# A graph layer on one core: edge groups of 8 columns, 5 gathered by Pool and 3 by TensorE, with window sums over 48 nodes

## The chip, the cores and the metric

The kernel runs on one core of a Trainium2 chip. The metric is the device time of one execution in microseconds. It is the median of the runs shown; a profiled execution of the same kernel gives the page and the trace.

## What is computed

There are 6250 nodes with 64 features and 206250 edges, sorted by the node that they point to. The features are normalized and cut at zero (h). Every edge takes the row of h at its source node, adds its own attributes and cuts at zero; the results are summed by destination, and a small two-layer network works on h plus the sum.

```python
h = jnp.maximum(_layernorm(x, axis=-1), 0.0)
msg = jax.nn.relu(h[src] + edge_attr)
agg = jax.ops.segment_sum(msg, dst, num_segments=x.shape[0])
y = h + agg
y = jax.nn.relu(y @ W1 + b1)
out = x + (y @ W2 + b2)
```

## The kernel before

**Groups.** The sorted edges are cut into groups of 128 x G edges, G = 6: a group is a tile of 128 partitions by 6 columns by 64 features. There are NG = 268 whole groups and a tail of four columns. For each edge two things are needed: the row of h at its source, and the place of its destination.

**Two ways to get the source rows.** Of each group the first G - H = 3 columns are gathered by Pool: one indirect DMA a column (`gather`, L175) brings 128 rows from `h_rows` in HBM into `xg`. The last H = 3 columns are fetched by TensorE from a copy of h that stays in SBUF (`hp`, three bf16 parts whose sum is the f32 value). It works in sets of two groups and in two steps. In the first (`slots_of`, L417), 56 matmuls a group select the wanted nodes of each of 28 parts into 32 slots a part, with the three parts side by side, 192 columns; ScalarE casts the result from PSUM to bf16 (`slots_out`, L425, tile `picked`). In the second (`pick`, L434), the way back, matmuls with the one-hot tile `backs` put each slot's row at its edge. Each of the 3 columns takes 7 x 3 = 21 matmuls of 64 columns, since the three parts are accumulated one after the other into the same 64 columns of PSUM. The one-hot tiles are made by VectorE (`find` L394, `back` L403) from tables that SP's queue loads (`source_load`, `spot_load`).

**One group's sum.** `messages(g)`: VectorE adds the gathered rows to the attributes (L478) and the picked rows to the other columns (L480); ScalarE cuts at zero (L482). `one_hot(g)` compares the edges' destinations with the W = 32 nodes that follow the group's first one (L464). `window_sum(g)` multiplies messages and one-hot on TensorE (L492) into a slice of the PSUM tile `agg`; one such tile holds AB = 4 groups and two tiles take turns. `sum_into_z(g)` adds the slice into z on VectorE, at an address read from the destinations (L458).

**Order.** The order of the work is written out by hand. After a start in which h is made (x is loaded, normalized, turned, split into parts) while RAW = 5 groups are gathered as raw rows of x and normalized by themselves, `half(g)` is called for every later group. Each call issues, in this order: the loads of group g + AHEAD (SP's queue for the attributes, Pool for the gathers; the pool of buffers holds LOOK = 12 groups, AHEAD = 9), a table load, `window_sum(g-1)`, the first part of `slots_of` for the next set, `sum_into_z(g-2)` and the output blocks that have become ready, `messages(g)`, `pick(g+1)` for two columns, the rest of `slots_of`, `pick(g+1)` for the third, `one_hot(g)`, and the one-hot tiles and ranking for later sets. Each engine does its own part of that list in order and waits where it needs another's result. PSUM holds two tiles each of `pick`, `half`, `rows` and `agg`.

At the end, a loop over edges that did not fit a window or a slot runs if there are any (`all_windows`).

Of the kernel before, what the change touches and what calls it, by code (L numbers as in the profile page):

```python
# [9 lines left out]
F32 = mybir.dt.float32  # L10
# [5 lines left out]
ALU = mybir.AluOpType  # L16
AX = mybir.AxisListType
DVE = mybir.EngineType.DVE

N, E, D = 6250, 206250, 64  # L20
P = 128
G = 6
GE = P * G
NG = E // GE
TE = E - NG * GE
# [3 lines left out]
TD = TJ * P - (TE - P)  # L29
C = NG * G  # L30
CT = TJ + 1
CP = C + G
W = 32
WB = 512
R = 4
NB = N // (P * R)
TN = N - NB * P * R
EPS = 1e-5
LOOK = 12
AHEAD = 9  # L40
LAG = 2
AB = 4
RV = 16

H = 3
# [6 lines left out]
S = 32  # L52
Q = PARTS * S // P
XC = 14
RAW = 5
F0 = RAW
KS = (NG + 1 - F0) // 2
assert F0 + 2 * KS == NG + 1
# [11 lines left out]
def kernel(  # L70
# [14 lines left out]
    nc = tc.nc  # L85
    ctx.enter_context(tc.manual_schedule())

    const = ctx.enter_context(tc.tile_pool(name="const", bufs=1))
    edge = ctx.enter_context(tc.tile_pool(name="edge", bufs=LOOK))
    work = ctx.enter_context(tc.tile_pool(name="work", bufs=2))  # L90
    rank = ctx.enter_context(tc.tile_pool(name="rank", bufs=2))
    dram = ctx.enter_context(tc.tile_pool(name="dram", bufs=1, space=bass.MemoryType.DRAM))
    psum = ctx.enter_context(tc.tile_pool(name="psum", bufs=2, space=bass.MemoryType.PSUM))

    src_sb = const.tile([P, CP], I32, name="src_sb")
    dst_sb = const.tile([P, CP], I32, name="dst_sb")
    FIRST = (F0 + 2 * 2 * SETS) * G
    nc.sync.dma_start(out=src_sb[:, :FIRST], in_=src_main[:, :FIRST])
# [60 lines left out]
    h_rows = dram.tile([NP, D], F32, name="h_rows")  # L159
    z = const.tile([P, N + W], F32, name="z")  # L160
    nc.vector.memset(z[D:], 0.0)
    nc.vector.memset(z[:D, N:], 0.0)

    def attr_load(ea, g):
        if g < NG:
            nc.sync.dma_start(out=ea.rearrange("p j d -> p (j d)"),
                              in_=edge_attr[g * GE:(g + 1) * GE, :].rearrange("(p j) d -> p (j d)", j=G))
        else:
            nc.sync.dma_start(out=ea[:, G - CT:G - 1].rearrange("p j d -> p (j d)"),
                              in_=edge_attr[C * P:(C + TJ) * P, :].rearrange("(p j) d -> p (j d)", j=TJ))  # L170
            nc.sync.dma_start(out=ea[:, G - 1, :], in_=edge_attr[E - P:, :])

    def gather(xg, idx, n, rows):
        for j in range(n):
            nc.gpsimd.indirect_dma_start(  # L175
                out=xg[:, j, :], out_offset=None, in_=rows[:, :],
                in_offset=bass.IndirectOffsetOnAxis(ap=idx[:, j:j + 1], axis=0))

    def first_col(g):
        return 0 if g < NG else G - CT  # L180

    def pool_cols(g):
        return G - H if g >= F0 else G

    def load(g):
        ea = edge.tile([P, G, D], F32, name="ea")
        attr_load(ea, g)
        lo, hi = first_col(g), pool_cols(g)
        if g < RAW:
            xg = lnp.tile([P, G, D], F32, name="xr", bufs=RAW)  # L190
        else:
            xg = edge.tile([P, G - H, D], F32, name="xg")
        gather(xg[:, lo:], src_sb[:, g * G + lo:g * G + hi], hi - lo, x if g < RAW else h_rows)
        return ea, xg

    def cols_of(g):
        return slice(g * G + first_col(g), (g + 1) * G)

    loaded = [load(g) for g in range(RAW)]

# [139 lines left out]
    def find_left(i):  # L340
# [3 lines left out]
        nc.vector.tensor_scalar(lf, sl, 1.0, None, op0=ALU.is_lt)  # L344
        nc.vector.scalar_tensor_tensor(lf, sl, float(W), lf, op0=ALU.is_gt, op1=ALU.add)
        nc.vector.scalar_tensor_tensor(lf, dst_sb[:, lo:hi], 1.0, lf, op0=ALU.add, op1=ALU.mult)
# [22 lines left out]
    def window_start(g):  # L369
        if g % RV == 0:  # L370
            n = min(RV, NG + 1 - g)
            _, vals = nc.values_load_multi_w_load_instructions(
                dst_sb[0:1, g * G:(g + n - 1) * G + 1:G], engines=(DVE,), min_val=0, max_val=N - 1,
                skip_runtime_bounds_check_because="dst holds numbers of nodes")
            for k, v in enumerate(vals):
                starts[g + k] = v
        return starts.pop(g)

    backs, sources, spots, found, picked, halves, picks = {}, {}, {}, {}, {}, {}, {}

    def source_load(k):
        sources[k] = rank.tile([P, PARTS * 2 * S], I16, name="sources")
        nc.sync.dma_start(out=sources[k][:PP], in_=lines[k // SETS][k % SETS].rearrange("(o m) s -> o (m s)", o=1)
                          .to_broadcast([PP, PARTS * 2 * S]))
# [41 lines left out]

    def pick(g, cols):
        k, i = divmod(g - F0, 2)
        if cols[0] == 0:
            picks[g] = psum.tile([P, H, D], F32, name="pick", bufs=2)  # L430
        for u in cols:
            for q in range(Q):
                for t in range(3):
                    nc.tensor.matmul(picks[g][:, u], backs[k][:, q, i * H + u, :],  # L434
                                     picked[k][:, i * Q + q, t * D:(t + 1) * D],
                                     start=(q == 0 and t == 0), stop=(q == Q - 1 and t == 2))

    def norm_edges(xg):
        s = work.tile([P, G], F32, name="raw_s")
# [11 lines left out]
        nc.vector.scalar_tensor_tensor(xg, xg, 0.0, v.unsqueeze(2).to_broadcast([P, G, D]),  # L451
                                       op0=ALU.max, op1=ALU.mult)

    aggs, hots, taken, msgs, banks = {}, {}, {}, {}, []

    def sum_into_z(g):
        at = window_start(g)
        nc.vector.tensor_tensor(z[:, ds(at, W)], z[:, ds(at, W)], aggs.pop(g), ALU.add)  # L458

    def one_hot(g):  # L460
        lo = first_col(g)
        n = G - lo
        oh = work.tile([P, G, W], F32, name="oh")
        nc.vector.tensor_tensor(  # L464
            oh[:, lo:], slot[:, cols_of(g)].unsqueeze(2).to_broadcast([P, n, W]),
            slots[:, :W].unsqueeze(1).to_broadcast([P, n, W]), ALU.is_equal)
        hots[g] = oh

    def enter(g):
        if g <= NG and g not in taken:  # L470
            taken[g] = loaded[g] if g < RAW else load(g)

    def messages(g):
        lo, m = first_col(g), pool_cols(g)
        ea, xg = taken.pop(g)
        if g < RAW:
            norm_edges(xg)
        nc.vector.tensor_tensor(ea[:, lo:m], ea[:, lo:m], xg[:, lo:m], ALU.add)  # L478
        if m < G:
            nc.vector.tensor_tensor(ea[:, m:], ea[:, m:], picks.pop(g), ALU.add)  # L480
        msg = work.tile([P, G, D], F32, name="msg", bufs=3)
        nc.scalar.activation(msg[:, lo:], ea[:, lo:], AF.Relu)  # L482
        msgs[g] = msg

    def window_sum(g):
        lo, oh, msg = first_col(g), hots.pop(g), msgs.pop(g)
        if g % AB == 0:
            banks.append(psum.tile([P, AB, W], F32, name="agg", bufs=2))
        pa = banks[-1][:, g % AB]
        for j in range(lo, G):  # L490
            i = (j - lo) % 2
            nc.tensor.matmul(pa[i * D:(i + 1) * D], msg[:, j, :], oh[:, j, :], start=(j < lo + 2), stop=(j >= G - 2))  # L492
        aggs[g] = pa
# [55 lines left out]
    def is_set(k):  # L549
        return 0 <= k < KS  # L550

    def half(g):
        k, i = divmod(g - F0, 2)
        first = ((0, 2), (8, 10))[i]
        later = ((4, 6), (12,))[i]
        now = is_set(k + 1)
        enter(g + AHEAD)
        if i == 0:
            if is_set(k + 3):
                source_load(k + 3)  # L560
        elif is_set(k + 3):
            spot_load(k + 3)
        if g >= 1:
            window_sum(g - 1)
        if now:
            for n0 in first:
                slots_of(k + 1, n0)
                slots_out(k + 1, n0)
        if g >= LAG:
            sum_into_z(g - LAG)  # L570
            blocks_behind(g - LAG)
        messages(g)
        if g < NG:
            pick(g + 1, (0, 1))
        if now:
            for n0 in later:
                slots_of(k + 1, n0)
                slots_out(k + 1, n0)
        if g < NG:
            pick(g + 1, (2,))  # L580
        one_hot(g)
        if i == 0:
            if is_set(k + 1):
                back(k + 1, 4, Q)
            if is_set(k + 2):
                find(k + 2, 0)
        else:
            if is_set(k + 2):
                back(k + 2, 0, 4)
                find(k + 2, 1)  # L590
        at = g - F0
        chunk(at + 14, rank_at)
        chunk(at + 13, rank_count)
        chunk(at + 12, rank_of)
        chunk(at + 11, rank_marks)
        chunk(at + 11, rank_turn)
        chunk(at + 10, rank_holds)
        chunk(at + 10, rank_fits)
        chunk(at + 9, source)
        if g in CHECKS:  # L600
            find_left(CHECKS.index(g))
# [50 lines left out]
    rank_fits(0)  # L652
    for g in range(AHEAD):
        enter(g)
# [4 lines left out]
    for g in range(RAW):  # L659
        enter(g + AHEAD)  # L660
        messages(g)
# [30 lines left out]
        slots_out(0, n0)  # L692
    source_load(2)
    spot_load(2)
    pick(F0, (0, 1, 2))
    find(1, 0)
    find(1, 1)
    back(1, 0, 4)
# [25 lines left out]
    with tc.If(any_left > 0):  # L724
        with tc.For_i(0, NG, 1) as i:
# [4 lines left out]
            ea = edge.tile([P, G, D], F32, name="ea")  # L730
# [5 lines left out]
        ea = edge.tile([P, G, D], F32, name="ea")  # L736
# [46 lines left out]
```

## Time and profile before

| | |
|---|---|
| Median of 3 runs | 2159.18 us (2152.33 to 2159.98) |
| Profiled execution | 2166.87 us |
| Span of its instructions | 2165.2 us |
| Mean granted clock of TensorE | 0.81 |
| Busy: PE, PEld | 1587.4, 1246.3 us |
| Busy: DVE, ACT, POOL | 964.1, 598.1, 864.5 us |
| Matmuls | 35792 |
| Instruction fetch queue q8 | 282 transfers, 4.62 MB |

PE is TensorE's matmuls and PEld its weight loads, which overlap them; DVE is VectorE, ACT ScalarE, POOL GpSimd, SP the engine whose queue issues most loads. The span runs from the first instruction to the last. In a row of the profile stand the line of the code, the engine and operation, the tiles written and read, the shapes and the count; then busy time and the mean of one in ns; then the idle time of the engine just before these instructions and what ended most of it. "Issue" as the end of a wait means that the profile shows nothing that was waited for. Matmuls are pipelined, so the mean of one (207 ns for L434) is a latency and not the pace of a stream; the pace is read from how long a row of many takes in the timeline.

### The profile page before, as it was taken

The numbers are of one execution on the slowest core, as the hardware profiler recorded it, in microseconds if no ns is written. First come the engines' busy times: TensorE is split into PE (matmuls) and PEld (weight loads), VectorE is DVE, ScalarE is ACT, GpSimd is POOL, SyncE is SP. The second block draws the span as 40 slices with busy tenths as digits, with TensorE's granted clock in tenths as the row PEclk, the third lists the DMA queues.
The fourth block names the chain that finished last, engine by engine and source line by source line (L and its number), as shares of the span: only waits on it lengthen the run. The fifth ranks groups of instructions, "written<-read, shape, count | busy, mean of one in ns | idle before, by whom it ended". The sixth has DMA issues, their size and how long they took to land.

```text
span 2165.2 us, 79562 instructions
## 1 busy us (share of the span) xinstructions
PE 1587.4 (73%) x35792; PEld 1246.3 (58%) x35792; DVE 964.1 (45%) x2721; ACT 598.1 (28%) x1351; POOL 864.5 (40%) x834
## 2 busy tenths in 40 slices
PE   1147787787778777777787778778777777778788
PEld 0135565565556655665565666556665566556566
DVE  7074443444444344444344444444444444444445
ACT  1132222232223222223222223222222322223223
POOL 7514433434444344434433443344434434443330
PEclk9998887777878788878778778777778987888779
DMA  5113233223333233333322323232323322323321
GB/s 165 29 47 88 73 95 81 71 75 83 78 81 88 80 74 77 88 79 88 83 72 76 88 72 90 75 85 74 89 71 82 96 76 70 89 77 91 81 77 35
DMA packets 112983, 172.67 MB, mean 80 GB/s; under 512 B 29185, under 2 KB 83585, under 8 KB 112637
## 3 DMA queue, kind: packets, MB, share of 16 engines
q1 hardware_dynamic: 85534, 139.02, 21.8%
q0 software_dynamic: 26240, 26.92, 7.5%
q8 instruction: 282, 4.62, 0.9%
q10 hardware_dynamic: 864, 1.60, 0.2%
q14 instruction: 63, 0.52, 0.1%
HBM read 163.56 MB, written 3.88 MB: 77 GB/s over the span
## 4 chain that ended last, share of the span: by engine, by line
PE 71%; issue 21%; another core or an unknown queue 3%; DVE 2%; DMA 2%; ACT 0%; DVEq 0%; POOL 0%; SPq 0%; ACTq 0%
PE pick L434 34%; PE half L417 25%; PE agg L492 8%; DMA x_sb<-in_x_dram 1%; PE rows L279 1%; PE rows L509 1%; PE rows L240 1%; PE rows L238 1%; PE rows L520 1%; PE rows L267 0%; DVE backs L403 0%; ACT z L318 0%; DVE found L394 0%; DVE rest L325 0%
## 5 line engine op out<-in xcount | busy, mean ns | idle before, releaser
L175 POOL DMA_INDIRECT xg<-h_rows,src_sb x790 | 831.1, 1052 | 1227.2 <-DVE ea L480 907.1
L434 PE MATMUL pick<-picked,backs 128*128 128x64 bf16 x16632 | 773.6, 207 | 245.3 <-issue 239.0
L434 PEld LDWEIGHTS <-backs 128*128 128x128 bf16 x16632 | 650.9, 107 | 412.4 <-issue 401.7
L425 ACT CAST picked<-half 128x384 bf16<-128x384 f32 x924 | 420.6, 480 | 1380.6 <-PE half L417 888.9
L417 PE MATMUL half<-hp,found 112*32 112x192 bf16 x14784 | 595.2, 283 | 196.9 <-issue 186.6
L417 PEld LDWEIGHTS <-found 112*32 112x32 bf16 x14784 | 379.6, 109 | 304.0 <-issue 267.7
L458 DVE TENSOR_TENSOR z<-z,agg 128x32 f32 x269 | 49.9, 185 | 714.1 <-PE agg L492 694.0
L403 DVE TENSOR_SCALAR backs<-spots,ids 128x768 bf16<-128x768 int16 x924 | 327.7, 414 | 0.0
L480 DVE TENSOR_TENSOR ea<-ea,pick 128x192 f32<-128x192 f32 x264 | 92.2, 349 | 407.7 <-PE pick L434 380.8
L492 PE MATMUL agg<-oh,msg 128*64 128x32 f32 x3224 | 187.9, 256 | 10.6 <-issue 8.1
L492 PEld LDWEIGHTS agg<-oh,msg 128*64 128x64 f32 x3224 | 153.2, 172 | 44.1 <-issue 27.8
L394 DVE TENSOR_SCALAR found<-sources,nodes_of 112x1792 bf16<-112x1792 int16 x264 | 178.0, 675 | 0.1
L482 ACT ACTIVATE msg<-ea 128x384 f32<-128x384 f32 x269 | 142.7, 530 | 5.3 <-DVE ea L478 3.0
L464 DVE TENSOR_TENSOR oh<-slot,slots 128x192 f32<-128x192 int16 x269 | 94.4, 351 | 0.0
L478 DVE TENSOR_TENSOR ea<-ea,xg 128x192 f32<-128x192 f32 x264 | 93.6, 355 | 0.7
L317 PE MATMUL rows<-ident,x_sb 112*64 112x112 f32 x56 | 12.7, 394 | 49.9 <-issue 42.5
L238 PE MATMUL rows<-at,upper 128*128 128x504 bf16 x44 | 25.7, 585 | 22.8 <-DVE at L232 21.5
L317 PEld LDWEIGHTS rows<-ident,x_sb 112*64 112x64 f32 x56 | 7.7, 160 | 55.2 <-issue 45.9
L279 PE MATMUL rows<-holds,marks 128*28 128x32 bf16 x792 | 29.5, 185 | 11.3 <-DVE holds L257 5.9
L175 POOL DMA_INDIRECT xr<-in_x_dram,src_sb x30 | 31.1, 1035 | 10.6 <-issue 8.8
L279 PEld LDWEIGHTS <-marks 128*28 128x28 bf16 x792 | 24.2, 100 | 15.5 <-DVE holds L257 6.0
L257 DVE TENSOR_TENSOR holds<-rank_of,from 128x576 bf16<-128x576 f32 x44 | 32.9, 749 | 0.0
(94 smaller groups left out, 391.3 us busy)
## 6 DMA issues: line engine op xcount, KB each, us to landing
sources<-source_row SPq DMA_DIRECT2D x132, 392.0 KB
ea<-in_edge_attr_dram SPq DMA_DIRECT2D x268, 192.0 KB
spots<-spot_rows SPq DMA_DIRECT2D x132, 192.0 KB
xg<-h_rows,src_sb POOLq DMA_INDIRECT x790
h_rows<-x_sb SPq DMA_DIRECT2D x4, 392.0 KB
x_sb<-in_x_dram SPq DMA_DIRECT2D x4, 388.5 KB
xb<-in_x_dram SPq DMA_DIRECT2D x12, 128.0 KB
out_dram<-o SPq DMA_DIRECT2D x12, 128.0 KB
```

The source lines that it names most:

```text
L175: nc.gpsimd.indirect_dma_start(out=xg[:, j, :], out_offset=None, in_=rows[:, :], in_offset=bass.IndirectOffsetOnAxis(ap=idx[:, j:j + 1], a ...
L279: nc.tensor.matmul(ps[:, i], mk[:, i * H + t, :], oh[:, i * H + t, :], start=(t == 0), stop=(t == H - 1))
L394: nc.vector.tensor_scalar(found[k][:PP, b].rearrange("p m i s -> p (m i s)"), sources[k][:PP], nodes_of[:PP, b:b + 1], None, op0=ALU.is_equal)
L403: nc.vector.tensor_scalar(backs[k][:, q].rearrange("p t s -> p (t s)"), spots[k].bitcast(I16), ids[:, q:q + 1], None, op0=ALU.is_equal)
L417: nc.tensor.matmul(ps[j * S:(j + 1) * S, u], found[k][:PP, b, m, i, :], hp[:, b * PARTS + m].rearrange("p t d -> p (t d)"), start=(b == 0) ...
L425: nc.scalar.copy(picked[k][:, n0:n0 + 2], halves.pop((k, n0)))
L434: nc.tensor.matmul(picks[g][:, u], backs[k][:, q, i * H + u, :], picked[k][:, i * Q + q, t * D:(t + 1) * D], start=(q == 0 and t == 0), st ...
L464: nc.vector.tensor_tensor(oh[:, lo:], slot[:, cols_of(g)].unsqueeze(2).to_broadcast([P, n, W]), slots[:, :W].unsqueeze(1).to_broadcast([P, ...
L478: nc.vector.tensor_tensor(ea[:, lo:m], ea[:, lo:m], xg[:, lo:m], ALU.add)
L480: nc.vector.tensor_tensor(ea[:, m:], ea[:, m:], picks.pop(g), ALU.add)
L482: nc.scalar.activation(msg[:, lo:], ea[:, lo:], AF.Relu)
L492: nc.tensor.matmul(pa[i * D:(i + 1) * D], msg[:, j, :], oh[:, j, :], start=(j < lo + 2), stop=(j >= G - 2))
```

## The change

Groups have 8 columns: NG becomes 201, with the same tail of four columns. Pool gathers 5 columns of each group and TensorE still fetches 3. The window is 48 nodes wide. Four groups are raw. LOOK is 9 and AHEAD 6.

On the way back, the three bf16 parts are no longer accumulated into the same columns: one matmul of 192 columns puts them side by side, so 7 matmuls serve a column. A PSUM tile of `pick` now has four blocks of 64 for each of two columns; ScalarE copies the edge attributes into the fourth (`room`), and VectorE sums the four blocks by a reduction that writes the attribute tile. A group uses two such tiles (two columns and one), and three take turns. The window sums of eight groups share the one PSUM tile `bank`.

```diff
-G = 6
+G = 8
-W = 32
+W = 48
-LOOK = 12
-AHEAD = 9
+LOOK = 9
+AHEAD = 6
-AB = 4
+AB = 8
-RAW = 5
+RAW = 4
...
     def pick(g, cols):
         k, i = divmod(g - F0, 2)
-        if cols[0] == 0:
-            picks[g] = psum.tile([P, H, D], F32, name="pick", bufs=2)
+        ps, lo = picks[g][len(picks[g]) - 2 + (cols[0] > 0)]
         for u in cols:
             for q in range(Q):
-                for t in range(3):
-                    nc.tensor.matmul(picks[g][:, u], backs[k][:, q, i * H + u, :],
-                                     picked[k][:, i * Q + q, t * D:(t + 1) * D],
-                                     start=(q == 0 and t == 0), stop=(q == Q - 1 and t == 2))
+                nc.tensor.matmul(ps[:, u - lo, :3].rearrange("p t d -> p (t d)"), backs[k][:, q, i * H + u, :],
+                                 picked[k][:, i * Q + q], start=(q == 0), stop=(q == Q - 1))
+
+    def room(g):
+        ea, m = taken[g][0], G - H
+        picks[g] = []
+        for lo, n in ((0, 2), (2, 1)):
+            ps = psum.tile([P, 2, 4, D], F32, name="pick", bufs=3)
+            nc.scalar.copy(ps[:, :n, 3], ea[:, m + lo:m + lo + n])
+            picks[g].append((ps, lo))
...
-    aggs, hots, taken, msgs, banks = {}, {}, {}, {}, []
+    aggs, hots, taken, msgs = {}, {}, {}, {}
+    bank = psum.tile([P, AB, W], F32, name="agg", bufs=1)
...
         if m < G:
-            nc.vector.tensor_tensor(ea[:, m:], ea[:, m:], picks.pop(g), ALU.add)
+            for (ps, at), n in zip(picks.pop(g), (2, 1)):
+                nc.vector.tensor_reduce(ea[:, m + at:m + at + n], ps[:, :n].rearrange("p j t d -> p j d t"), AX.X, ALU.add)
...
-        if g % AB == 0:
-            banks.append(psum.tile([P, AB, W], F32, name="agg", bufs=2))
-        pa = banks[-1][:, g % AB]
+        pa = bank[:, g % AB]
...
         messages(g)
         if g < NG:
+            room(g + 1)
             pick(g + 1, (0, 1))
...
-    pick(F0, (0, 1, 2))
+    room(F0)
+    pick(F0, (0, 1))
+    pick(F0, (2,))
```

## The prediction

> **What bounds the kernel now.** I read the page first, its chain of waits and its costliest groups.
>
> ```profile
> PE 71%; issue 21%; another core or an unknown queue 3%; DVE 2%; DMA 2%; ACT 0%; DVEq 0%; POOL 0%; SPq 0%; ACTq 0%
> ...
> L175 POOL DMA_INDIRECT xg<-h_rows,src_sb x790 | 831.1, 1052 | 1227.2 <-DVE ea L480 907.1
> L434 PE MATMUL pick<-picked,backs 128*128 128x64 bf16 x16632 | 773.6, 207 | 245.3 <-issue 239.0
> ...
> L458 DVE TENSOR_TENSOR z<-z,agg 128x32 f32 x269 | 49.9, 185 | 714.1 <-PE agg L492 694.0
> ```
>
> TensorE holds the chain, and 21% of the span (455 us) is "issue": TensorE stands still and waits for nothing that the profile names. So I asked where this lies. Cut at the window sums, a timeline gives the 264 pipelined steps ("halves" in the code), from 145 to 2157 us: 2012 us, 7.62 us each. Four of them in the view by windows (length, then busy us and count of PE, PEld, DVE, ACT, POOL, then TensorE's granted clock):
>
> ```profile
> 896.15:901.81 5.66, 5.66 (x140) 5.02 (x139) 2.92 (x7) 2.24 (x5) 0.00 (x0) 0.68 0.13 38
> 901.81:908.52 6.71, 4.93 (x127) 3.53 (x125) 3.51 (x10) 1.76 (x4) 3.05 (x3) 1.00 0.09 17
> 908.52:913.57 5.05, 4.41 (x140) 3.74 (x140) 3.36 (x10) 2.23 (x6) 3.11 (x3) 1.00 0.58 162
> 913.57:925.04 11.47, 6.53 (x146) 4.58 (x143) 3.60 (x12) 2.00 (x5) 6.78 (x7) 0.79 0.18 45
> ```
>
> The matmuls are equally many; what differs is Pool, with none, three, three and six gathers (a seventh row overlaps). Without gathers TensorE has no gap; with six the half is twice as long. Over all halves from the 40th the means are 6.2, 7.1, 6.5 and 11.2 us, the gaps 0.1, 1.6, 0.8 and 4.6. Runs of three gathers hold 1.3 us of gaps, runs of six 4.6, and outside them (up to 1.5 us after) there is none. One run of six in the timeline (start, us, row, idle before):
>
> ```profile
> 889.05 0.27 PE L417 MATMUL half<-hp,found 112*32 112x192 bf16 x2 [0.43 <-issue]
> 889.79 0.34 PE L417 MATMUL half<-hp,found 112*32 112x192 bf16 x6 [0.46 <-issue]
> ...
> 890.14 0.94 POOL L175 DMA_INDIRECT xg<-h_rows,src_sb  x1 [0.30 <-issue]
> 890.55 0.31 PE L434 MATMUL pick<-picked,backs 128*128 128x64 bf16 x5 [0.41 <-issue]
> ...
> 891.39 0.95 POOL L175 DMA_INDIRECT xg<-h_rows,src_sb  x1 [0.30 <-issue]
> 891.99 0.28 PE L434 MATMUL pick<-picked,backs 128*128 128x64 bf16 x4 [1.14 <-issue]
> ...
> 893.44 0.38 PE L434 MATMUL pick<-picked,backs 128*128 128x64 bf16 x4 [0.54 <-issue]
> ```
>
> Matmuls drip in fives: about 31 in 6.9 us, 4.5 a us, on average over 58 runs of six, against 27 before. The drip begins some 1.5 us after the first gather, as if about 38 matmuls were already taken in, and ends 0.9 us after the last. So **TensorE is starved of instructions while Pool gathers**; the rows show that it happens, not why. After the long runs the clock also halves. Prices at half clock (first three) and full clock (last three):
>
> ```profile
> 614.99 0.86 PE L492 MATMUL agg<-oh,msg 128*64 128x32 f32 x12
> 615.78 1.47 PE L417 MATMUL half<-hp,found 112*32 112x192 bf16 x32
> 617.18 2.42 PE L434 MATMUL pick<-picked,backs 128*128 128x64 bf16 x42
> ...
> 621.19 0.54 PE L492 MATMUL agg<-oh,msg 128*64 128x32 f32 x12
> 621.66 0.84 PE L417 MATMUL half<-hp,found 112*32 112x192 bf16 x32
> 622.44 1.40 PE L434 MATMUL pick<-picked,backs 128*128 128x64 bf16 x42
> ```
>
> That is 45 ns (full) and 72 (half) for a window sum, 26 and 46 for L417, 33 and 58 for L434.
>
> **The change, part by part.** *Fewer halves.* 206250 edges make 201 groups of 1024 in place of 268 of 768, and 198 halves (groups 4 to 201) in place of 264. What a half does per set of three TensorE columns stays: 56 L417 matmuls, 3.5 casts on ScalarE, 3.5 compares for backs and one for found on VectorE. 66 of each go. The halves must average under (2165.2 - 153.2)/198 = 10.16 us to win, 153.2 us being what lies before 145 and after 2157. I leave that as it is: four raw groups of eight columns (32 gathers) replace five of six (30).
>
> *Wide picks.* 63 matmuls of 64 columns become 21 of 192. Weight loads already lie under the streams, so I price by columns: 3 x 33 = 100 ns and 3 x 58 = 174, 2.1 or 3.65 us a half, as much as now. L238's 504 columns begin 0.39 us before the next row at half clock, 0.77 ns a column against 58/64 = 0.9, so at best 15% less. What falls is the count, which matters where instructions are scarce.
>
> *Window sums.* 16 records of 48 columns in place of 12 of 32: 16 x 45 = 0.72 us if width were free, 1.08 if it counts in full; I take 0.9 (half clock 1.45).
>
> So a half's matmuls go from 12+56+63+4 = 135 to 16+56+21+4 = 97 (the 4 is ranking, 22 matmuls per six halves). Its own time was 0.54+1.46+2.08+0.28+0.13 (ranking, output blocks) = 4.5 us at full clock and 7.7 at half; it becomes 0.9+1.46+2.1+0.28+0.17 = 4.9 and 8.3.
>
> *Pool.* 5 gathers a half in place of 3: 197 x 5 + 1 = 986 for 790. A run of three lasts 4.0 us, of six 7.4, so five 6.3; nothing on Pool is late at 9 us a half. Were they to slip like the 1.9 us rows, a run would last 7. But the runs starve TensorE. Now VectorE's z sum (L458) waits for the window sum issued just before, though it reads the earlier group's slice: tile agg is ordered as a whole. Only where a new agg tile begins, each fourth group, does VectorE go ahead, release xg early, and two runs of three merge into one of six. With one agg tile for everything that exception ends, and I expect five gathers each half.
>
> *VectorE.* The add grows from 192 to 320 elements (355 ns; 558 for 384 at L478's wide form: 490). The sum with pick, 349, becomes reduces over 512 and 256 inputs; L447 takes 548 for 384, so 690 and 410. The rows show no strided read of PSUM; by twice that price 2.2 us. One-hot grows from 351 to 555. VectorE has 3.6 us a half now, some 4.9 after, under 9: off the path except for the next part.
>
> *ScalarE and a new wait.* Two copies a half into PSUM: by 255 ns (L269, 128 elements) and 0.3, 0.45 us. Relu grows from 530 to 640. The copies write the pick tiles that the matmuls then fill; ordered as a whole like agg, the first pick waits for ScalarE, which waits behind relu of the group before, which waits for VectorE's reduces. From a half's start: window sum 0.9, z and add 0.55, reduces 1.05, relu 0.65, first copy 0.25: 3.4 us. TensorE has 0.9 + 32 x 26 ns = 1.7 us of work ahead of it, so it stands about 1.7 us (1.2 at half clock, whose matmuls take longer). Behind the waiting pick stand the later L417 matmuls and so ScalarE's casts. From below: nothing, if the columns are ordered apart. I count the stall as hidden: Pool's run begins at 1.4 us, TensorE cannot be fed faster afterwards anyway, and what it holds meanwhile is used later. If that cover were gone it would cost up to 1.7 x 198 = 337 us.
>
> *Loads.* 99 sets in place of 132 take 33 x 584 KB off SP's queue; LOOK and AHEAD keep six groups of eight ahead, 48 columns for 54. Priced at nothing: nothing on the chain waits for a landing now.
>
> *The sum.* A half: run 6.3 + 0.9 = 7.2 us; in it 38 matmuls held, then 5.7 x 4.5 = 26; the other 33 at full supply. At a clock as now (41% of the time half: 61 ns each) 2.0 us: 9.2. The same reckoning for four halves of today (runs 3, 3, 6) gives 18.1 us of runs, 114 + 61 matmuls in them, 365 more at 40 ns, 32.7 us in all against 30.5 measured; it is 7% high. So 8.6 to 9.2; I take 8.9: 198 x 8.9 + 153 = 1915 us against a span of 2165.2. The runs shown lie some 6 us below their profiled one (2159.18 to 2166.87): **1910 us**.
>
> **Rivals** (times are spans). *The new wait adds to the starving* (slower). Gaps as in the rows, 1.3 for three and 4.6 for six, make 3.5 for five; own time at today's clock 5.9; if then 1.4 us of waiting for the copies is not covered, 10.8 us, 2290 us. It decides from 0.76 us uncovered on. For it: the chain is of one half, without slack. Against: the matmuls held in the meantime.
>
> *The clock stays at half.* Each half now has a starved stretch near 6 us, where today one in four has. 7.2 + 33 x 86 ns = 10.0: 2140 us. For it: the clock of 0.50 follows the runs of six. Against: runs of three leave 1.00. The Trainium skill, page "TensorE: Matmul & The Clock Gate", section on why this matters for your kernels, warns against "PE-idle gaps >~3µs between matmul bursts", after which the clock halves. By that rule the drip, whose gaps last 1.1 us, would not be such a gap; the trace halves all the same, so by the rows I keep this rival.
>
> *Runs of five do not starve.* A run of three still lets 14.7 matmuls a us through. Then 4.9 us of own time and a 1.7 us wait, or Pool's 5 x 1.38 = 6.9, set the pace: 7.0 us, 1540 us. Against: the drip of the longer runs.
>
> *It does more than it says*, the slow loop over left edges: 1024 sorted edges at 33 a node span about 31 nodes, under 48. No chance worth giving.
>
> **How the numbers follow.** Forecast 0.58 (7.6 to 9.8 us a half, 1660 to 2090), clock at half 0.11, added wait 0.19, no starving 0.12. A measurement of this kernel can tell about 0.5% from no change. Slower is the added wait's 0.19, same 0.04 taken from the clock's case (its 2140 lies 1% below the time before), faster 0.77. The range reaches from 1660 to 2190, where much of the added wait's and the fast case still lie outside.
>
> **What would show it.** "Issue" on the chain a smaller sum, about 3 us a half or less; Pool in even runs of five; no 4-half rhythm; pick's first matmul released by ScalarE's copy; 198 halves near 8.9 us. Halves over 10.2 us, or TensorE without gaps while Pool gathers, would make it wrong.

## The result, and the profile after

The changed kernel takes **1876.62 us** (median of 4 runs, 1870.79 to 1882.23) beside 2159.58 us of the kernel before: a ratio of 0.8695, 95% interval 0.8662 to 0.8728. The prediction was 1910 us, 1660 to 2190.

That holds for the chip that measured it, and not for every chip. The runs came in six jobs, each on a chip given to it; where the chip is on record, none came twice. What lies in the chip and what lies in anything else that is set once for a job can therefore not be told apart here, and "chip" below stands for both. In three of the jobs the kernel before took 2117 to 2160 us, in the other three 1345 to 1366; its runs within one job lie within 2% of each other. On one chip of the second kind the changed kernel takes 1458.20 us against 1344.99: a ratio of 1.0828 (1.0793 to 1.0862), **slower**. What the kernel does in the two cases is the subject of what follows; what differs between the chips was not found.

The page of the changed kernel, costliest groups (row, then busy us and mean ns, then idle time before and its end):

```profile
L175 POOL DMA_INDIRECT xg<-h_rows,src_sb x986 | 1034.4, 1049 | 727.2 <-DVE ea L484 477.5
L432 PE MATMUL pick<-picked,backs 128*128 128x192 bf16 x4158 | 566.4, 302 | 414.6 <-ACT pick L440 376.9
...
L417 PE MATMUL half<-hp,found 112*32 112x192 bf16 x11088 | 410.2, 287 | 49.3 <-issue 45.2
...
L487 DVE TENSOR_REDUCE ea<-pick 128x128 f32<-128x512 f32 (+1 forms) x396 | 201.1, 549 | 0.0
L489 ACT ACTIVATE msg<-ea 128x512 f32<-128x512 f32 x202 | 126.9, 628 | 80.7 <-DVE ea L487 77.8
...
L484 DVE TENSOR_TENSOR ea<-ea,xg 128x320 f32<-128x320 f32 x198 | 97.2, 491 | 8.0 <-DMA xg<-h_rows,src_sb 1.2
L440 ACT COPY pick<-ea 128x128 f32<-128x128 f32 (+1 forms) x396 | 79.1, 233 | 0.0
```

The chain on that page is followed back over some 3% of the span only, so TensorE's gaps are counted in the trace. The idle time before the picks, once put down to issue, now ends with ScalarE's copy (L440). One half of the changed kernel in its timeline (start, us, row, idle before; the weight loads and SP are left out):

```profile
1011.30 0.90 PE L417 MATMUL half<-hp,found 112*32 112x192 bf16 x32
1011.31 0.21 DVE L464 TENSOR_TENSOR z<-z,agg 128x48 f32 x1 [1.38 <-PE agg L497]
...
1011.59 0.49 DVE L484 TENSOR_TENSOR ea<-ea,xg 128x320 f32<-128x320 f32 x1
...
1012.00 1.01 DVE L487 TENSOR_REDUCE ea<-pick 128x128 f32<-128x512 f32 x2
...
1012.35 0.94 POOL L175 DMA_INDIRECT xg<-h_rows,src_sb  x1 [2.69 <-DVE ea L484]
...
1013.04 0.63 ACT L489 ACTIVATE msg<-ea 128x512 f32<-128x512 f32 x1 [0.32 <-DVE ea L487]
...
1013.58 0.40 ACT L440 COPY pick<-ea 128x128 f32<-128x128 f32 x2
...
1013.89 1.31 PE L432 MATMUL pick<-picked,backs 128*128 128x192 bf16 x14 [1.70 <-ACT pick L440]
```

The chain is the one foretold: z, add, reduces, relu, copy, pick. TensorE is done with its 32 L417 matmuls at 1012.2 and stands 1.70 us. Pool's run of gathers begins at 1012.35, inside that wait.

All runs that have a trace, in one table. "Half" is the time from the first pick to the end of the last, over 264 halves of the kernel before and its variants or 198 of the changed one. The last two columns are TensorE's gaps over 150 ns in that stretch, put down to issue and to ScalarE's copy; all in us. "Before there" is the kernel before in the same job.

| kernel | before there | time | half | issue gaps | waits for the copy |
|---|---|---|---|---|---|
| before | 2159.6 | 2159.6 | 7.62 | 441 | 0 |
| changed | 2159.6 | 1876.6 | 8.64 | 152 | 377 |
| e12, copies early | 2125.8 | 1815.6 | 8.27 | 360 | 1 |
| e5, before, plain loads by SP | 2117.2 | 1317.8 | 4.56 | 65 | 0 |
| e8, before, plain loads by Pool | 2117.2 | 1338.3 | 4.63 | 82 | 0 |
| e7, before, Pool computes | 2117.2 | 1563.2 | 5.51 | 14 | 0 |
| e6, changed, plain loads by SP | 2117.2 | 1438.2 | 6.71 | 0 | 351 |
| e4, before, one sum tile | 1347.6 | 1341.8 | 4.69 | 80 | 0 |
| e9, changed again | 1345.0 | 1458.2 | 6.82 | 0 | 358 |
| e3, changed, narrow picks | 1347.6 | 1466.8 | 6.86 | 1 | 357 |
| e1, changed, no copies | 1347.6 | 1406.5 | 6.55 | 0 | 0 |
| e2, copies early | 1347.6 | 1393.6 | 6.44 | 0 | 1 |
| e10, copies early | 1345.0 | 1394.7 | 6.39 | 0 | 1 |
| e11, copies early | 1366.2 | 1397.5 | 6.41 | 0 | 1 |

### The profile page after: what moved, and what is told of

The parts are those of the page before. It is cut to its first block, busy times and chain, and to the rows that moved or that the text cites. A ratio compares the mean times of both kernels' runs of the same rounds, so it can differ in the third digit from the quotient of the medians.

```text
span 1880.5 us, 45735 instructions
## 1 busy us (share of the span) xinstructions
PE 1201.4 (64%) x19380; PEld 921.8 (49%) x19380; DVE 951.0 (51%) x2272; ACT 554.4 (29%) x1425; POOL 1069.2 (57%) x1032
## 5 line engine op out<-in xcount | busy, mean ns | idle before, releaser
L175 POOL DMA_INDIRECT xg<-h_rows,src_sb x986 | 1034.4, 1049 | 727.2 <-DVE ea L484 477.5
L432 PE MATMUL pick<-picked,backs 128*128 128x192 bf16 x4158 | 566.4, 302 | 414.6 <-ACT pick L440 376.9
L432 PEld LDWEIGHTS <-backs 128*128 128x128 bf16 x4158 | 451.1, 119 | 519.7 <-issue 494.9
L425 ACT CAST picked<-half 128x384 bf16<-128x384 f32 x693 | 316.0, 480 | 1034.6 <-PE half L417 636.7
L417 PE MATMUL half<-hp,found 112*32 112x192 bf16 x11088 | 410.2, 287 | 49.3 <-issue 45.2
L417 PEld LDWEIGHTS <-found 112*32 112x32 bf16 x11088 | 270.6, 109 | 141.9 <-issue 125.4
L497 PE MATMUL agg<-oh,msg 128*64 128x48 f32 x3224 | 194.0, 244 | 79.6 <-issue 78.3
L487 DVE TENSOR_REDUCE ea<-pick 128x128 f32<-128x512 f32 (+1 forms) x396 | 201.1, 549 | 0.0
L489 ACT ACTIVATE msg<-ea 128x512 f32<-128x512 f32 x202 | 126.9, 628 | 80.7 <-DVE ea L487 77.8
L470 DVE TENSOR_TENSOR oh<-slot,slots 128x384 f32<-128x384 int16 x202 | 110.5, 547 | 0.0
L484 DVE TENSOR_TENSOR ea<-ea,xg 128x320 f32<-128x320 f32 x198 | 97.2, 491 | 8.0 <-DMA xg<-h_rows,src_sb 1.2
L440 ACT COPY pick<-ea 128x128 f32<-128x128 f32 (+1 forms) x396 | 79.1, 233 | 0.0
L317 PE MATMUL rows<-ident,x_sb 112*64 112x112 f32 x56 | 12.8, 394 | 61.9 <-issue 45.3
L317 PEld LDWEIGHTS rows<-ident,x_sb 112*64 112x64 f32 x56 | 7.7, 160 | 67.2 <-issue 48.1
```

What stands on the lines that cost most here:

```text
L175: nc.gpsimd.indirect_dma_start(out=xg[:, j, :], out_offset=None, in_=rows[:, :], in_offset=bass.IndirectOffsetOnAxis(ap=idx[:, j:j + 1], a ...
L417: nc.tensor.matmul(ps[j * S:(j + 1) * S, u], found[k][:PP, b, m, i, :], hp[:, b * PARTS + m].rearrange("p t d -> p (t d)"), start=(b == 0) ...
L425: nc.scalar.copy(picked[k][:, n0:n0 + 2], halves.pop((k, n0)))
L432: nc.tensor.matmul(ps[:, u - lo, :3].rearrange("p t d -> p (t d)"), backs[k][:, q, i * H + u, :], picked[k][:, i * Q + q], start=(q == 0), ...
L440: nc.scalar.copy(ps[:, :n, 3], ea[:, m + lo:m + lo + n])
L470: nc.vector.tensor_tensor(oh[:, lo:], slot[:, cols_of(g)].unsqueeze(2).to_broadcast([P, n, W]), slots[:, :W].unsqueeze(1).to_broadcast([P, ...
```

## The experiments

e1 to e4 ran in one job, e5 to e8 in the next, then e9 with e10, and e11 and e12 each alone.

**e5: is it Pool's gathers?** In the kernel before, for the groups of the pipelined part:

```diff
-        gather(xg[:, lo:], src_sb[:, g * G + lo:g * G + hi], hi - lo, x if g < RAW else h_rows)
+        if g < RAW:
+            gather(xg[:, lo:], src_sb[:, g * G + lo:g * G + hi], hi - lo, x)
+        else:
+            for j in range(lo, hi):
+                r0 = (g * G + j) % (N // P) * P
+                nc.sync.dma_start(out=xg[:, j, :], in_=h_rows[r0:r0 + P, :])
```

> The kernel before with each gather of the pipelined groups replaced by a plain load of 128 neighbouring rows of h, issued by SP: the same bytes into the same tiles, the wrong rows. Pool has nothing to do there. Theory (Pool's gathers starve TensorE of instructions): hardly any issue on TensorE's chain, 264 halves of 5 to 6.2 us, 1470 to 1790 us. Rival (instruction fetch or transfers of any kind starve it): 2100 to 2170 us with the same share of issue.

Measured: 1317.77 us, 0.626 (0.606 to 0.647) of the kernel before on the same chip, where that took 2117. A half takes 4.56 us in place of 7.62. Its page, the chain and two groups:

```profile
PE 86%; issue 6%; DVE 4%; DMA 2%; ACT 1%; DVEq 1%; ACTq 0%; SPq 0%
...
L439 PE MATMUL pick<-picked,backs 128*128 128x64 bf16 x16632 | 588.9, 194 | 18.8 <-issue 18.3
L422 PE MATMUL half<-hp,found 112*32 112x192 bf16 x14784 | 420.5, 250 | 42.9 <-issue 34.6
```

In the kernel before, the second group was this:

```profile
L417 PE MATMUL half<-hp,found 112*32 112x192 bf16 x14784 | 595.2, 283 | 196.9 <-issue 186.6
```

The matmuls are the same 16632 and 14784. Issue is 6% of the chain in place of 21%, and the idle time before the picks 18.8 us in place of 245.3; the granted clock is 0.99 in place of 0.81. The time fell below the range I had given (1470): a half takes 4.56 us where I had 5 at the least, and what lies outside the halves takes 106 us in place of 153. So the gathers cost the kernel before some 800 us on that chip. Instruction fetch is not short in itself: the same 282 transfers came within a span of 1311 us in place of 2165.

**e8: any DMA of Pool, or the indirect kind?** The same edit with `nc.gpsimd.dma_start` in place of `nc.sync.dma_start`.

> The kernel before with each gather of the pipelined groups replaced by a plain load of 128 neighbouring rows issued from Pool's own queue, the wrong rows. If any DMA that Pool makes starves TensorE: gaps in step with Pool's instructions, 1900 to 2200 us. If only the indirect kind does: as with loads by SP, 1470 to 1790 us.

Measured: 1338.25 us, 0.636 (0.616 to 0.656), again below the range foretold and beside e5. Its page:

```profile
L198 POOL DMA_DIRECT2D xg<-h_rows x790 | 538.6, 688 | 689.4 <-DVE ea L485 598.2
...
L439 PE MATMUL pick<-picked,backs 128*128 128x64 bf16 x16632 | 592.8, 194 | 53.0 <-issue 52.2
```

Pool issues as many DMAs of as many packets (26240 on its queue in both kernels), 688 ns each in place of 1052, and TensorE has 82 us of issue gaps in place of 441. It takes the indirect kind, or what comes with it: these loads read neighbouring rows where the gathers read scattered ones, and the two were not separated.

**e7: or Pool's being busy?** Each gather becomes a memset of the column and an iota of 1024 elements into a scratch tile.

```diff
+            for j in range(lo, hi):
+                nc.gpsimd.memset(xg[:, j, :], 0.0)
+                nc.gpsimd.iota(busy, pattern=[[1, 1024]], base=1, channel_multiplier=0,
+                               allow_small_or_imprecise_dtypes=True)
```

> The kernel before with each gather of the pipelined groups replaced by two computing instructions of Pool, a memset of the tile's column and an iota of 1024 elements into a scratch tile, together about as long as a gather (near 1 us); no rows are loaded there and the column is zero. Theory (it is the gather's DMA that starves TensorE, not that Pool is busy): no issue gaps, 1470 to 1790 us. Rival (a busy Pool slows TensorE's instructions): 2050 to 2200 us.

Measured: 1563.24 us, 0.743 (0.721 to 0.765), with 14 us of issue gaps. Pool was as busy (927 us) and starved nobody; what takes the time here is something else, in the groups of this kernel:

```profile
L411 DVE TENSOR_SCALAR backs<-spots,ids 128x768 bf16<-128x768 int16 x924 | 863.5, 991 | 0.0
L200 POOL IOTA busy<- 128x1024 f32 x790 | 833.9, 1056 | 0.0
...
L425 PE MATMUL half<-hp,found 112*32 112x192 bf16 x14784 | 465.3, 263 | 210.4 <-DVE found L402 205.7
```

VectorE's compares for backs take 991 ns in place of 414, and TensorE waits for found, which VectorE makes behind them. The 751 compares that overlap an instruction of Pool take 1126 ns on average, the 173 that overlap none 404. The Trainium skill, page "SBUF — State Buffer", section on who interferes with whom, has VectorE's two-port modes and GpSimd lock each other out of a shared pair of ports; these compares agree with it.

**e6: the changed kernel without gathers.** The edit of e5 in the changed kernel.

> The changed kernel with the same replacement: rows are loaded by SP, the wrong ones, and Pool is idle. Theory: own time 4.9 and the wait for ScalarE's copies, 1.7 to 2 us, set a half: 198 halves of 6 to 7 us, 1350 to 1540 us; the wait on the copies is then the largest one. Rival: 1850 to 1890 us.

Measured: 1438.17 us, 0.684 (0.664 to 0.704), a half of 6.71 us, no issue gaps, and 351 us of waits for ScalarE's copy. Without starving e5, the kernel before without gathers, is 120 us faster. The wait is the largest of TensorE's and long enough to account for that, but it was not taken out of this kernel.

**e9: the changed kernel where nothing starves.** The kernel before had taken 1347.6 us beside the first four experiments. The changed kernel, unaltered, was run again.

> The changed kernel, unaltered. The kernel before took 1347.6 us beside the first four experiments and 2117 us beside the next four, so what starves TensorE is not there on every chip. Theory (the change wins by issuing fewer instructions where Pool's gathers starve TensorE, and brings a wait for ScalarE's copies of its own): where the kernel before takes near 2150 us, 1860 to 1890 us; where it takes near 1350, the wait decides and the changed kernel is slower, 1400 to 1480 us. Rival (the change is a gain of its own kind): 0.87 of the kernel before in either case.

Measured: 1458.20 us, 1.083 (1.079 to 1.086) of the kernel before, at the same chip's 1344.99. Its page:

```profile
L175 POOL DMA_INDIRECT xg<-h_rows,src_sb x986 | 1034.5, 1049 | 304.9 <-issue 252.7
L432 PE MATMUL pick<-picked,backs 128*128 128x192 bf16 x4158 | 512.8, 284 | 358.5 <-ACT pick L440 358.5
...
L417 PE MATMUL half<-hp,found 112*32 112x192 bf16 x11088 | 345.6, 271 | 2.8 <-issue 2.5
```

Here Pool gathers nearly without a pause, 0.3 us between almost any two, and TensorE has no issue gaps: 2.8 us before L417 in place of 49.3. The gathers are as long as on the first chip (1049 ns in both). So the same instruction starves TensorE on one chip and not on another. Two things speak against the change in these rows: a wait of 1.8 us a half, and Pool, whose five gathers take 5 x (1.05 + 0.30) = 6.75 us of a half of 6.82. The kernel before has 4.69 us a half (e4); 198 halves may take 264 x 4.69/198 = 6.25 to be even. The granted clock is lower too, 0.86 to 0.88 in the three middle stretches of 300 us, where e4 has 0.97 to 0.98.

**e1 and e2: without the wait, where nothing starves.** e1 leaves out ScalarE's copies; VectorE sums three blocks and adds. e2 keeps them and issues them at the start of the half, with room for it in PSUM:

```diff
         enter(g + AHEAD)
+        if g < NG:
+            room(g + 1)
...
         messages(g)
         if g < NG:
-            room(g + 1)
             pick(g + 1, (0, 1))
...
-            ps = psum.tile([P, 2, 4, D], F32, name="pick", bufs=3)
+            ps = psum.tile([P, 2, 4, D], F32, name="pick", bufs=4)
```

and one PSUM tile for `rows` in place of two.

> The changed kernel without ScalarE's copies into the pick tiles: VectorE sums three blocks into a small tile and adds it to the attributes, two small adds more a half. The first pick no longer waits for ScalarE (1.98 us a half in the changed kernel's waits). Theory (the wait lies beside Pool's run, and instructions are what is short): 1.83 to 1.90 ms, at most 3% under the changed kernel's 1876.6 us; gaps put down to issue take the place of the wait. Rival (the wait comes on top): 1.4 to 1.98 us a half less, 198 halves, 1480 to 1600 us.

> The changed kernel with ScalarE's copies moved to the start of a half, ahead of its casts, four pick tiles in place of three and one PSUM tile for rows in place of two. The copies stay, the wait goes. Theory: as for the kernel without the copies, 1.82 to 1.90 ms. Rival (the wait comes on top): 1480 to 1600 us. If VectorE's two small adds matter instead, this one and the one without copies differ by over 2%.

Measured: 1406.52 us, 1.042 (1.036 to 1.047), and 1393.61 us, 1.032 (1.027 to 1.036) of the kernel before. These two can't be set against 1876.6 us, and so tell nothing on the question that they were made for. Against e9 by ratio, they are 4 to 5% faster. e1 did not free TensorE: it waits 174 us for VectorE's reduce to let go of a pick tile (L486). One repeat of e2, beside e9, and another on a further chip:

> The changed kernel with ScalarE's copies at the start of a half and four pick tiles, as in the second experiment. Where the kernel before takes near 1350 us: 1387 to 1400 us again. Where it takes near 2150 us: theory of the prediction (the wait lies beside Pool's run) 1.82 to 1.90 ms, rival (the wait comes on top) 1480 to 1600 us.

> The changed kernel with ScalarE's copies at the start of a half and four pick tiles once more, for a chip on which the kernel before takes near 2150 us. There, theory of the prediction (the wait for the copies lies beside Pool's run, and instructions are short): 1.82 to 1.90 ms. Rival (the wait comes on top of the starving): 1480 to 1600 us. Where the kernel before takes near 1350 us: 1387 to 1400 us as in the second and tenth experiments, Pool without a pause.

Measured: 1394.72 us, 1.037 (1.033 to 1.040), and 1397.51 us, 1.023 (1.018 to 1.028), where the kernel before took 1344.99 and 1366.22. Still slower than the kernel before. With the wait gone, VectorE's add waits for the rows (L484 for DMA, 283 us in e10), and Pool sets the pace; the chain of e10:

```profile
POOL 34%; DMA 28%; issue 17%; DVE 13%; PE 6%; ACT 1%; DVEq 0%; POOLq 0%; SPq 0%; ACTq 0%
```

Pool's 1018 gathers follow one another there from 5.8 to 1370.2 us, 0.3 us apart. That alone is longer than the 1345 us of the kernel before, which has 820 of them: on such a chip five gathers a group are too many, whatever is done about the wait.

**e12: without the wait, where TensorE starves.** The kernel of e2 once more, this time beside a kernel before of 2125.82 us.

> The same kernel a last time, for the same question. Where the kernel before takes near 2150 us: 1.82 to 1.90 ms if the wait for the copies lies beside Pool's run, 1480 to 1600 us if it comes on top of the starving. Where it takes near 1350 us: 1387 to 1400 us.

Measured: 1815.59 us, 0.8525 (0.8486 to 0.8564). That is 4 us under the range foretold for a kernel before near 2150 us, and over 200 above the rival's. By ratio that is 2.0% under the changed kernel (0.8525/0.8695 = 0.980), from two jobs, each against its own kernel before. 377 us of waits went, some 2% of the time came back. What took their place, in the waits (us in total, times, longest) of the changed kernel and of this one:

```profile
PE half L417 <- issue: 45.2, 111, 2.5
```

```profile
PE half L417 <- issue: 242.4, 517, 2.5
```

L417 waits 242 us for issue where the changed kernel has 45, all issue gaps 360 us where it has 152. In runs of five gathers alone, up to 1.5 us after them, they are 1.92 us a run where the changed kernel has 0.76. So most of the wait lay beside the starving: TensorE stood still for one reason or for the other. Part of the loss may be the rhythm: without the wait Pool's runs merge more often (26 of ten and five of fifteen, beside 121 of five), and what that costs was not measured apart. This is the fastest kernel here on such a chip that gathers its rows; on the other kind it loses 2 to 4% to the kernel before.

**e3: narrow picks.** The changed kernel with three matmuls of 64 columns for each of 192.

```diff
-                nc.tensor.matmul(ps[:, u - lo, :3].rearrange("p t d -> p (t d)"), backs[k][:, q, i * H + u, :],
-                                 picked[k][:, i * Q + q], start=(q == 0), stop=(q == Q - 1))
+                for t in range(3):
+                    nc.tensor.matmul(ps[:, u - lo, t], backs[k][:, q, i * H + u, :],
+                                     picked[k][:, i * Q + q, t * D:(t + 1) * D],
+                                     start=(q == 0 and t == 0), stop=(q == Q - 1 and t == 2))
```

> The changed kernel with each 192-column pick made as three of 64 columns into the same three blocks: 139 matmuls a half in place of 97, the same columns. Theory (the number of instructions is what Pool's gathers limit): some 1.5 us a half more, 2100 to 2250 us. Rival (columns are what costs): 1870 to 1930 us.

Measured: 1466.76 us, 1.0875 (1.0826 to 1.0925). It came to a chip that does not starve, so it answers only there: its interval and that of e9 (1.0793 to 1.0862) overlap, and no cost of 42 more matmuls a half is clear of noise, beside 357 us in which TensorE waits for the copy anyway. What the wide picks save under starving was not measured.

**e4: one sum tile in the kernel before.**

```diff
-    aggs, hots, taken, msgs, banks = {}, {}, {}, {}, []
+    aggs, hots, taken, msgs = {}, {}, {}, {}
+    bank = psum.tile([P, AB, W], F32, name="agg", bufs=1)
```

with AB = 8 and slices of `bank`, as in the change.

> The kernel before with one agg tile for eight groups in place of two for four each; nothing else. Theory (a fresh agg tile lets VectorE ahead each fourth half and merges two runs of gathers): runs of three in every half, no rhythm of four, gaps of 1.3 us a half in place of 1.75 on average, 2000 to 2100 us. Rival (the rhythm comes from elsewhere): 2150 to 2170 us with runs of three, three and six as before.

Measured: 1341.83 us, 0.995 (0.991 to 0.999), also where nothing starves. What the rhythm of four halves costs under starving stays open. The run is of use as a trace of the kernel before, but for that tile, on the other kind of chip. Its stretch of 600 to 900 us, beside that of the kernel before (length, then busy us and count of PE, PEld, DVE, ACT, POOL, granted clock, DMA share, GB/s), first e4's, then that kernel's:

```profile
600.00:900.00 300.00, 277.46 (x8544) 236.41 (x8536) 217.82 (x620) 133.34 (x311) 207.36 (x190) 0.97 0.47 132
```

```profile
600.00:900.00 300.00, 230.62 (x5153) 180.24 (x5149) 133.18 (x381) 82.70 (x189) 123.46 (x117) 0.80 0.32 83
```

8544 matmuls and 190 gathers in 300 us against 5153 and 117: more gathers in the same time, and no starving.

## Why the prediction was right, and where it was not

*What bounds the kernel* was right for this kind of chip. That the gathers do it is now shown and not only read off a rhythm: take them away (e5) and the issue gaps fall from 441 to 65 us and the half clock goes with them; plain DMAs from the same queue (e8) and a busy Pool (e7) leave TensorE fed. That instructions are what TensorE lacks is still a reading of the gaps.

*The number.* 198 halves of 8.64 us, where I took 8.9, are 51 us less; the rest of the span is 169.9 us, where I left 153.2, 17 us more; together the 35 us between 1915 and the span of 1880.5. Some 14 of the 17 are in the start, which I priced at nothing: the first L417 matmul comes at 151.7 us in place of 138.2. There Pool gathers 77 columns in one run where it had 66, and TensorE has issue gaps too (45 us before its transposes, L317). On the other kind of chip the first one comes at 88.8 us (e4 and e9). That the two differ in opposite ways is chance, and brought the sum closer than its parts.

*The terms of a half.* Add 491 ns (490 foretold), reduces 1.01 us for the pair (1.1), relu 628 ns (640), one-hot 547 ns (555), copies 0.40 us (0.45). The wide picks start 82 ns apart at full clock and 160 at half, where I took 100 and 174 from rows that include a tail. The wait is 1.90 us a half (377/198) where I took 1.7.

*The wait is hidden.* Right, within 2%: e12. A half of the changed kernel is 1.90 us of this wait, 0.77 of issue gaps and 6.0 of the rest; the rival had 1.4, 3.5 and 5.9. So the wait came in full, and the gaps shrank beside it. This was the step on which the slower rival hung: it gave that wait 1.4 us a half on top, and in e12 removing it would then have given 1480 to 1600 us.

*Even runs of five.* Right as a count: 168 runs of five and ten of ten in the changed kernel, and halves of 8.80, 8.77, 8.76 and 8.66 us by their place in four (the 40th to the 190th group), where the kernel before has 6.2, 7.1, 6.5 and 11.2. The reason I gave, the single agg tile, is not enough: e12 has the same tile, and its runs merge to ten and fifteen more often. What the single tile does in the kernel before under starving was not shown (e4).

*The clock.* 0.80 to 0.81 in the three middle stretches of 300 us, as before: the forecast's, and not the rival of a clock that stays at half.

*The law of supply*, 38 matmuls held and 4.5 a us while Pool gathers, gave 9.2 us, and 8.6 by the 7% that it is high for the kernel before; measured 8.64. It counts too few: in the 168 runs of five TensorE starts 73 matmuls from the first gather to 0.9 us after the last (7.4 us), where I had 64 in 7.2. That what is held during the wait is used later came as foretold. Hardly a matmul starts in the first 1.5 us of such a run, and the first issue gap (over 150 ns) comes 5.8 us after the first gather and after 65 matmuls, on average over 118 runs; the other 50 have none. In the runs of six of the kernel before it comes after 1.7 us and 39 matmuls. So the gaps do not begin at a set time of Pool's run, but when some number of matmuls is used up, which fits a want of instructions (the law gives 57 for the 65). That the number of instructions is what counts, and not their length, is not shown by itself: e3 came to the wrong kind of chip.

*What no step foresaw.* "The rows show that it happens, not why" was said of the starving, but I priced every case as if it happened wherever the kernel runs. In three of six jobs it does not. Where it is absent, "Runs of five do not starve" is what the changed kernel does, at 1458 us for 1540; but the kernel before then takes 1345, so a case that I had counted as the fastest is the one in which the change loses, by 8%.

## What to carry to other kernels

Idle time of an engine that the profile puts down to nothing should be laid beside the other engines' instructions: here it followed one kind of DMA on another engine. Such a bound may be there on one chip and not on another, so a change that trades work against it should be timed on several before it is called a gain. A wait that lies beside another stall can be large in the list of waits, 377 us here, and worth only 2% when it is removed.

## What the runs showed of the hardware that was not expected

While Pool issues indirect DMAs, TensorE on three of six jobs' chips comes down, after the first 38 or so, to some 4.5 matmuls with their weight loads in a us, in small lots about 0.73 us apart (runs of six in the kernel before); on the other three it goes on without such gaps, with gathers of the same length. The loss is 800 us of 2117 (e5). Plain DMAs of neighbouring rows from the same queue do not do it (e8). What differs between the chips was not found: the transfers of instructions take about as long on both kinds (1.11 us on average in the kernel before, 1.07 in e4). The Trainium skill, page "SBUF — State Buffer", section on who interferes with whom, says of SBUF's ports that "DMA never contends with a compute engine". No row here shows a wait for a port; the gathers cost TensorE its 800 us by some other way, and the supply of instructions is the likely one.

The start suffers as well: with Pool in its first run of gathers, the turning of h through TensorE and ScalarE ends at 105 us on such a chip (first line) and at 55.5 on the other (second, e4):

```profile
104.12 0.80 ACT L318 COPY z<-rows 64x448 f32<-64x448 f32 x2 [0.29 <-PE rows L317]
```

```profile
54.74 0.81 ACT L318 COPY z<-rows 64x448 f32<-64x448 f32 x2 [0.29 <-PE rows L317]
```
